# Another order of start, first batches and products in a graph layer kernel on one core

## The chip, the core and the metric

The kernel runs on one core of one Trainium2 chip. The metric is the device time of one execution in microseconds (us); smaller is better. The core has five engines that run beside one another and meet only at semaphores: TensorE (PE: matrix products and transposes, its weight loads shown as PEld), VectorE (DVE), ScalarE (ACT), GpSimd (POOL) and SyncE (SP), which here only starts transfers. ScalarE and GpSimd start transfers as well. A name with a q, as in SPq, is the queue of instructions of that engine.

## The reference

The input x has 32 batches of 512 tokens of 256 channels, and adj is a 512x512 mask for each batch. With h = relu(layernorm(x)), the layer computes

```
conv  = relu(h + bn2(conv17(relu(bn1(conv1x1(h))))))       # along the tokens
s     = h @ w_se.T + b_se                                   # 3 features a token
A     = exp(-|s_n - s_m|^2) * adj
nmp   = A @ relu(h @ w_msg.T + b_msg)
gi    = concat(conv, nmp) @ w_ih.T + b_ih ;  gh = h @ w_hh.T + b_hh
out   = x + GRU cell(gi, gh, h)
```

bn1 and bn2 are batch norms with given statistics, so each is one scale and one shift for a channel. All data are fp32.

## The kernel before

Batches are handled in two groups of 16 (GB = 16, NG = 2). The convolution of 17 taps is done in the frequency domain: windows of 64 tokens are turned into spectra of length 80, which gives UNITS = 40 units for each group, and a unit is a product of 128 windows by 256 channels with the transformed taps. The program has these stages in order.

**First part of group one** (`first_part(0, ...)`, up to about 174 us). For each batch: load x, `statistics` (mean and variance on VectorE, the power -0.5 on GpSimd, L290), `normalise` (VectorE, L296), `transpose_h` (TensorE transposes phT, L307, then VectorE writes hT with the relu, L308, and SyncE stores it), `conv1` (TensorE pc, L320; VectorE adds the shift, L323; ScalarE the relu, L324) and `windows_to_freq` (TensorE px, L335; ScalarE copies into xf, L338). Between these stand pieces of `weights_to_freq` (TensorE pw, L256; copies into wst on VectorE, L263, and ScalarE, L265), two for a batch, which transform the taps and store them in the DRAM tile WD, and one of `load_weights` for a batch. The last of these, `vectors`, forms the biases brz and the scale and shift of bn2 from the transfer vec2 that `load_vectors` started a batch before.

**Nodes of group one** (`nodes(0, ...)`, to about 469 us). It goes through the batches in the order `todo`. For each: `message` (TensorE pm, L431), `features` (VectorE, small), `factors` (TensorE transposes psl and psr, L450 and L455, copied by ScalarE), `affinity` (TensorE pd, L466; exp on ScalarE; transpose of adj and product on VectorE, L471 and L472) and `aggregate` (TensorE pn, L480). Units are spread among them: `product` (TensorE py, L385) needs the unit's weights wt (`load_unit`, L347, three buffers in the pool wts), their sum wsum (GpSimd, L351) and two combinations of the spectrum, both (GpSimd, L364 and L365). Its result y goes through ScalarE (L391) and VectorE (L392, L393) to DRAM. The last four units of group one (LEFT = 4), u0 to u3, are left for the next stage.

**First part of group two** (`first_part(1, ...)`, to about 590 us). The same steps for 16 more batches, without `weights_to_freq`. The four left units are done among its first batches: the list `left` has their steps, and each call of `fill()` takes one entry. `combine_weights` forms sums of the gate weights on GpSimd, one step a batch.

**Nodes of group two** (to about 891 us) is as in group one, with 40 units spread over 13 batches. **The gates**, from 891 us to the end, use pairs of batches and are not touched by the change.

The order of the instructions on each engine is what the program says where a stage stands under `tc.manual_schedule()`: the two first parts and the gates. In `nodes` the framework's scheduler puts the instructions of each engine in order. Every engine works through its own queue in that order, so an instruction that waits holds all that is behind it. PSUM has eight banks of 512 values, given out in turn by `bank()`; a product waits until whoever reads the bank's earlier contents is done.

The first batches of group one run on TensorE in this order (T transposes, C conv1, W a piece of weights_to_freq, F windows_to_freq; the number is the batch): T0 C0 W W T1, C1 T2 W F0 W, T3 C2 W F1 W, and so on. In group two: T0 u0 u1 C0 u2 T1 u3, T2 C1 F0, T3 C2 F1.

Of the kernel before, what the change touches and what calls it, by code (L numbers as in the profile page):

```python
# [11 lines left out]
FP = mybir.dt.float32  # L12
# [3 lines left out]
P = 128  # L16
# [49 lines left out]
def gnn_layer(  # L66
# [88 lines left out]
    def vectors():  # L155

        for h in range(2):
            rows = slice(64 * h, 64 * (h + 1))
            nc.vector.tensor_copy(vech[rows].rearrange("p (m e) -> p e m", e=DC),
                                  vec2[rows].rearrange("p e (m h) -> p e m h", h=2)[..., h])  # L160
        for name in VEC:
            at[name] = vech[:, cols[name]]
        nc.vector.tensor_add(brz, at["b_ih"][:, : 2 * DC], at["b_hh"][:, : 2 * DC])
        batch_norm("bn2", scale2, shift2, nc.vector)

    def batch_norm(k, scale, shift, engine):
        engine.tensor_scalar(scale, at[k + "_v"], BN_EPS, None, op0=ALU.add)
# [173 lines left out]

    WT, WSUM, BOTH = {}, {}, {}

    def load_unit(g, u):
        t = WT[g, u] = wts.tile([P, 2, DC, D], FP, tag="wt", name=f"wt_{g}_{u}")
        for k in range(2):
            nc.sync.dma_start(t[:, k], WD[2 * u + k, : D * D].rearrange("(p i o) -> p i o", i=DC, o=D))  # L347

# [150 lines left out]
    def combine_weights():  # L499

        steps = []
        for k, src in enumerate((w_hhT, w_ihT[D:], w_ihT[:D])):
            w, t = (pools["sums"].tile([P, n, 3 * P], FP, tag=f"w{n}", name=f"w{n}_{k}", bufs=m) for n, m in ((4, 1), (7, 2)))
            if k == 1:
                nc.sync.dma_start(w.rearrange("p (c h) m -> p c (h m)", c=DC), src.rearrange("(c p) m -> p c m", p=P))
            else:
                load_rows(w.rearrange("p (c h) m -> p c (h m)", c=DC), src, nc.sync)

            a11, a21, a12, a22 = (
                w[:, 2 * c : 2 * c + 2].rearrange("p h m -> p (h m)").rearrange("p (g i o) -> p g i o", i=2, o=32)[:, :, i]  # L510
                for c in range(DC) for i in range(2)
            )
            q = [t[:, n].rearrange("p (g o) -> p g o", o=32) for n in range(7)]
            for (dst, x1, x2, op), kept in zip(
                ((Q5, a21, a22, ALU.add), (Q6, q[Q5], a11, ALU.subtract),
                 (Q7, a11, a21, ALU.subtract), (Q3, a12, q[Q6], ALU.subtract)),
                ((Q1, a11), (Q2, a12), (Q4, a22), None),
            ):
                steps.append([partial(nc.gpsimd.tensor_tensor, q[dst], x1, x2, op=op)])
                if kept:  # L520
                    steps[-1].append(partial(nc.scalar.copy, q[kept[0]], kept[1]))
            steps[-1].append(partial(nc.sync.dma_start, WS[k], t.rearrange("p q (g o) -> p q g o", o=P)))
        return steps
# [275 lines left out]
    def first_part(g, freq, between, left=()):  # L799


        b0, b1 = g * GB, (g + 1) * GB
        for b in range(b0, b0 + 3):
            if b not in X and (g == 0 or b == b0):
                load_x(b)
        if g == 0:
            t = XN[b0] = pools["first"].tile([P, NC, D], FP, tag="xn", name="rows", bufs=2)
            ones, diags = t[:, 0, :P], t[:, 1:3, :].rearrange("p i (c m) -> p i c m", m=P)
            nc.vector.memset(ones, 1.0)
            batch_norm("bn1", scale1, shift1, nc.gpsimd)  # L810
            bn1_row(0, scale1, ones, diags)
            bn1_row(1, shift1, ones, diags)
        if b0 not in STATS:
            statistics(b0)
        normalise(b0)
        if g == 0:
            scale_w1()
            shift_w1()
        else:
            load_x(b0 + 1)  # L820
            load_x(b0 + 2)
        left = list(left)

        def fill():
            for step in left.pop(0) if left else ():
                step()

        fill()
        transpose_h(b0)
        fill()  # L830
        statistics(b0 + 1)
        normalise(b0 + 1)
        fill()
        for b in range(b0, b1):
            if b + 3 < b1:
                load_x(b + 3, nc.gpsimd)
            if b == b0:
                conv1(b)
                if g == 0:
                    for steps in between(0):  # L840
                        for step in steps:
                            step()
                fill()
            if g == 0 and b == b0 + 1:
                conv1(b)
            if b + 2 < b1:
                statistics(b + 2)
            if b + 1 < b1:
                transpose_h(b + 1)
            if b + 2 < b1:  # L850
                normalise(b + 2)
            if b == b0:
                fill()
                xf = freq(g)
            one, two = between(b - b0) if b > 0 else ([], [])
            if b > b0 + (g == 0):
                conv1(b)
            if b == b1 - 1:
                load_h(b0)
            for step in one:  # L860
                step()
            if b > b0:
                windows_to_freq(b - 1, xf)
            for step in two:
                step()
        by_chunks(b1 - 1)
        load_h(b0 + 1)
        windows_to_freq(b1 - 1, xf)
        by_chunks(b0)
        return xf  # L870
# [8 lines left out]
    with tc.tile_pool(name="freq", bufs=1) as fpool:  # L879
# [27 lines left out]
        def nodes(g, xf, units, last):  # L907


            b1 = (g + 1) * GB  # L910
            todo = [b1 - 1] + list(range(g * GB, b1 - 1))
            def begin(i):
                if i < GB:
                    if todo[i] not in HQ:
                        by_chunks(todo[i])
                    message(todo[i])
                    features(todo[i])

            load_adj(todo[0])
            begin(0)  # L920
            factors(todo[0])
            begin(1)
            affinity(todo[0])
            for i, b in enumerate(todo):
                mine = spread(units, i, last) if i < last else []
                more = i + 1 < GB

                if g + 1 < NG and i == GB // 2:
                    load_x(b1)
                if g + 1 < NG and i == 3 * GB // 4:  # L930
                    statistics(b1)
                if i + 2 < GB and todo[i + 2] not in HT:
                    load_h(todo[i + 2])
                if more:
                    load_adj(todo[i + 1])
                    factors(todo[i + 1])
                for u in mine[:1]:
                    product(pools["pw"], g, u, xf)
                begin(i + 2)
                if more:  # L940
                    affinity(todo[i + 1])
                for u in mine[1:2]:
                    product(pools["pw"], g, u, xf)
                aggregate(b)
                save_nmp(b)
                for u in mine[2:]:
                    product(pools["pw"], g, u, xf)

        with phase("pw", "ahead"):
            with phase("nodes"):  # L950
                nodes(0, xf, range(UNITS - LEFT), GB)
            with phase("first", "sums"):
                combine = combine_weights()

                def between(b):

                    if b == GB - 3:
                        for u in range(3):
                            load_unit(1, u)
                    two = [partial(sum_unit, pools["pw"], 1, b - GB + 3)] if b > GB - 3 else []  # L960
                    return combine[b - 2] if 1 < b < len(combine) + 2 else [], two


                pw, (u0, u1, u2, u3) = pools["pw"], range(UNITS - LEFT, UNITS)
                left = [[partial(load_unit, 0, u2)],
                        [partial(prepare, pw, 0, u1, xf), partial(product, pw, 0, u0, xf)],
                        [partial(product, pw, 0, u1, xf), partial(load_unit, 0, u3), partial(prepare, pw, 0, u2, xf)],
                        [partial(prepare, pw, 0, u3, xf), partial(product, pw, 0, u2, xf)],
                        [partial(product, pw, 0, u3, xf)]]
                prepare(pw, 0, u0, xf)  # L970
                load_unit(0, u1)
                with tc.manual_schedule():
                    xf = first_part(1, freq_tile, between, left)
            with phase("nodes"):
                nodes(1, xf, range(UNITS), GB - 3)
# [76 lines left out]
```

## Time and profile before

The median of three runs is 1853.91 us (1850.42 to 1854.76). The profiled execution has a span of 1857.3 us.

| stage | us of the span | PE idle in it, us | where |
|---|---|---|---|
| start to first conv1 | 0 to 11.5 | 8.1 | 7.24 before L187, 0.82 before L320 |
| rest of first part, group one | 11.5 to 174 | 4.9 | 2.12 at 20, 0.56 at 34, 1.82 and 0.32 at 88 to 92 |
| nodes, group one | 174 to 469 | 3.4 | all before 230 |
| first part, group two | 469 to 590 | 3.7 | 2.32 at 479, 1.35 at 489 |
| nodes, group two | 590 to 891 | 2.8 | 1.01 at 594, 0.71 at 607 |
| gates | 891 to 1857 | 9.5 | in the last 80 us |

The page has for each engine its busy time. The granted clock (PEclk) is a share of TensorE's full clock; it is 1.00 nearly everywhere. The timeline's columns are start, duration, engine, line, operation, output and inputs with their shapes, number of instructions, and in brackets how long the engine had been idle and what ended that wait. TensorE's matrix products of fp32 stand in the records twice each, and their durations overlap: a product with 512 columns takes 0.86 us by the distance of its neighbours.

### The profile page before, as it was taken

What the parts mean: (1) busy time and instruction counts of PE and PEld (TensorE: products, weight loads), DVE (VectorE), ACT (ScalarE), POOL (GpSimd) and SP (SyncE); (2) the same over time, 40 slices, a digit from 0 to 9 for tenths busy, and PEclk for the clock granted to TensorE, in tenths of its full rate; (3) what the DMA queues carried; (4) which work ended last, traced back from release to release, by engine and by line L of the source; (5) the groups of instructions that cost most, each with busy time, mean ns of one, the idle gap of its engine ahead of it and who ended that gap; (6) DMA issues with size and microseconds to landing.
All of it is one profiled execution on the core that took longest, in us unless ns stands there. A gap on an engine that the chain in (4) does not pass through costs nothing.

```text
span 1857.3 us, 20078 instructions
## 1 busy us (share of the span) xinstructions
PE 1824.6 (98%) x6598; PEld 1088.2 (59%) x6598; DVE 1112.3 (60%) x2234; ACT 578.5 (31%) x1075; POOL 587.3 (32%) x565
## 2 busy tenths in 40 slices
PE   7999999999999999999999999999999999999998
PEld 5667666666798667666555544555455544555443
DVE  7775565555696554555165566645665466645666
ACT  3455434342245433333222211222122212222121
POOL 3322243344442344444412322132213322132221
PEclk9989999999999999999999999999999999999999
DMA  8988989865677988768512442244422442244312
GB/s 227 296 244 239 219 231 252 214 185 180 202 240 209 240 244 243 220 199 249 159 61 58 119 119 85 42 111 119 113 65 61 119 119 85 41 112 119 110 25 52
DMA packets 307451, 289.25 MB, mean 156 GB/s; under 512 B 148028, under 2 KB 237148, under 8 KB 306964
## 3 DMA queue, kind: packets, MB, share of 16 engines
q1 hardware_dynamic: 281300, 224.22, 45.6%
q10 hardware_dynamic: 19024, 38.68, 5.8%
q0 software_dynamic: 7024, 25.07, 4.9%
q8 instruction: 53, 0.87, 0.2%
q14 instruction: 50, 0.41, 0.1%
HBM read 191.50 MB, written 96.40 MB: 155 GB/s over the span
## 4 chain that ended last, share of the span: by engine, by line
PE 91%; DVE 3%; DMA 3%; issue 2%; POOL 1%; ACT 1%; SPq 0%; POOLq 0%; ACTq 0%; DVEq 0%
PE pg L585 29%; PE pn L585 14%; PE pn L480 11%; PE py L385 11%; PE pc L320 5%; PE pm L431 5%; PE pc L573 5%; PE px L335 3%; PE pw L256 2%; PE pd L466 2%; PE phT L307 1%; DMA hT<-hd 1%; PE psr L455 1%; DMA nd<-nmp 0%; DVE stats L284 0%
## 5 line engine op out<-in xcount | busy, mean ns | idle before, releaser
L480 PE MATMUL pn<-A,msg 128*128 128x512 f32 x512 | 225.1, 593 | 0.0
L585 PE MATMUL pg<-hp,sw 128*128 128x512 f32 x434 | 221.8, 593 | 0.7 <-DVE rz L604 0.5
L585 PE MATMUL pg<-cp,sw 128*128 128x512 f32 x434 | 221.6, 592 | 0.0
L585 PE MATMUL pg<-np,sw 128*128 128x512 f32 x434 | 221.6, 592 | 0.0
L563 POOL TENSOR_TENSOR hp<-hp 128x512 f32<-128x512 f32 x64 | 81.0, 1276 | 412.9 <-DMA hp<-hd 263.9
L364 POOL TENSOR_TENSOR both<-xf 128x256 f32<-128x256 f32 x78 | 60.1, 771 | 326.6 <-PE py L385 293.3
L480 PEld LDWEIGHTS pn<-A,msg 128*128 128x128 f32 x512 | 97.3, 190 | 110.8 <-issue 107.7
L385 PE MATMUL py<-wt,both 128*128 128x256 f32 x624 | 152.8, 388 | 3.0 <-POOL both L365 2.3
L563 POOL TENSOR_TENSOR cp<-cp 128x512 f32<-128x512 f32 x64 | 80.5, 1269 | 233.8 <-ACT cp L579 232.5
L600 ACT ACTIVATE rz<-rz,brz 128x512 f32<-128x512 f32 x93 | 67.0, 721 | 260.2 <-DVE rz L604 260.2
L392 DVE TENSOR_TENSOR y<-y,py 128x256 f32<-128x256 f32 x78 | 31.8, 408 | 193.3 <-ACT y L391 191.0
L585 PEld LDWEIGHTS pg<-hp,sw 128*128 128x128 f32 x434 | 82.2, 190 | 104.8 <-issue 97.8
L585 PEld LDWEIGHTS pg<-np,sw 128*128 128x128 f32 x434 | 82.5, 190 | 103.8 <-issue 103.8
L585 PEld LDWEIGHTS pg<-cp,sw 128*128 128x128 f32 x434 | 82.5, 190 | 103.8 <-issue 103.8
L385 PEld LDWEIGHTS py<-wt,both 128*128 128x128 f32 x624 | 115.4, 192 | 46.1 <-issue 27.6
L472 DVE TENSOR_TENSOR A<-e,at 128x512 f32<-128x512 f32 x128 | 113.5, 925 | 33.2 <-ACT e L469 33.0
L351 POOL TENSOR_TENSOR wsum<-wt 128x512 f32<-128x512 f32 x78 | 109.5, 1405 | 54.0 <-DMA wt<-wd 44.6
L320 PE MATMUL pc<-w,hT 128*128 128x256 f32 x512 | 120.8, 391 | 2.9 <-DVE hT L308 2.9
L723 ACT ACTIVATE nt<-nt,vech 128x512 f32<-128x512 f32 x64 | 46.2, 722 | 235.8 <-DVE nt L722 235.8
L431 PE MATMUL pm<-wmsg,hq 128*128 128x259 f32 x512 | 117.6, 381 | 1.3 <-ACT hq L417 1.0
L585 PE MATMUL pn<-np,sw 128*128 128x512 f32 x224 | 114.4, 592 | 0.0
L585 PE MATMUL pn<-hp,sw 128*128 128x512 f32 x224 | 114.4, 592 | 0.0
(141 smaller groups left out, 2954.5 us busy)
## 6 DMA issues: line engine op xcount, KB each, us to landing
wt<-wd SPq DMA_DIRECT2D x160, 256.0 KB, 4.2
adj<-in_adj_dram SPq DMA_DIRECT2D x128, 256.0 KB, 5.8
wd<-wst SPq DMA_DIRECT2D x64, 320.0 KB, 5.3
yd<-y ACTq DMA_DIRECT2D x80, 256.0 KB, 4.4
yt<-yd SPq DMA_DIRECT2D x30, 640.0 KB, 7.3
hd<-hT SPq DMA_DIRECT2D x32, 512.0 KB, 4.2
nd<-nmp ACTq DMA_DIRECT2D x32, 512.0 KB, 3.5
xb<-in_x_dram SPq DMA_DIRECT2D x128, 128.0 KB, 3.8
```

The costliest lines, as they stand in the source:

```text
L320: nc.tensor.matmul(p[:, j, :], HT[b][:, ic, c * P : (c + 1) * P], w1[:, ic, :], start=(ic == 0), stop=(ic == DC - 1))
L335: nc.tensor.matmul(p[:, j * 2 * L : (j + 1) * 2 * L], H1[b][:, c0 + j, ic * P : (ic + 1) * P], fwd, start=True, stop=True)
L351: nc.gpsimd.tensor_tensor(t, WT[g, u][:, 0], WT[g, u][:, 1], op=ALU.add)
L364: nc.gpsimd.tensor_tensor(both[:, 0], re, im, op=ALU.add)
L385: nc.tensor.matmul(dst, v[:, ic, :], w[:, ic, :], start=(ic == 0), stop=(ic == DC - 1))
L431: nc.tensor.matmul(p[:, : D + NS], hq[:, ic, c * P : (c + 1) * P], wmsg[:, ic, :], start=(ic == 0), stop=(ic == DC - 1))
L472: nc.vector.tensor_mul(A[b][:, mc, :], e, at)
L480: nc.tensor.matmul(p, MSG[b][:, mc, dc * P : (dc + 1) * P], A[b][:, mc, :], start=(mc == 0), stop=(mc == NC - 1))
L563: nc.gpsimd.tensor_tensor(t[:, dst, :], t[:, a, :], t[:, b, :], op=sub)
L573: nc.tensor.matmul(bk[:, t0:t1], YT[p][j][:, c, oc * P : (oc + 1) * P], back[:, n : n + t1 - t0], start=(c == 0), stop=(c == len(spans) - ...
L585: nc.tensor.matmul(bk[:, t], sw[:, k, q, o, :], terms[k][q][:, t], start=(first and i == 0), stop=(i == len(ks) - 1), skip_group_check=True)
L600: nc.scalar.activation(rz[:, g, j, :], src, AF.Sigmoid, bias=brz[:, g : g + 1], scale=1.0)
```

## The change

It has five parts, all about the order of work:

- `vectors` runs on GpSimd instead of VectorE.
- In front of the first real products, six matrix products of constants (ident and the zero tile fr) are issued on TensorE; their result is overwritten.
- In the first two batches of group one, the pieces of `weights_to_freq` and the work on VectorE are put in another order: T0 C0 W T1, C1 W T2 W F0 W, and hT of batch 1 stands before the statistics of batch 2.
- In the first part of group two, the steps of the left units move: the third unit's weights get a tile in the pool sums and are loaded between two loads of x, it is prepared before the second unit's product, and conv1 stands ahead of the next batch's transposes from the second batch on. The loads of the gate weights become steps of their own in `combine_weights`, which then start one batch earlier.
- In `nodes`, the first unit's product stands between the first batch's message and factors, and the other units are spread as before.

All of it is meant to keep TensorE supplied in places where it waits, and to have its clock up when the real work starts. The same instructions run as before, but for the six products in front.

```diff
--- before.py
+++ after.py
@@ -156,12 +156,12 @@
 
         for h in range(2):
             rows = slice(64 * h, 64 * (h + 1))
-            nc.vector.tensor_copy(vech[rows].rearrange("p (m e) -> p e m", e=DC),
+            nc.gpsimd.tensor_copy(vech[rows].rearrange("p (m e) -> p e m", e=DC),
                                   vec2[rows].rearrange("p e (m h) -> p e m h", h=2)[..., h])
         for name in VEC:
             at[name] = vech[:, cols[name]]
-        nc.vector.tensor_add(brz, at["b_ih"][:, : 2 * DC], at["b_hh"][:, : 2 * DC])
-        batch_norm("bn2", scale2, shift2, nc.vector)
+        nc.gpsimd.tensor_add(brz, at["b_ih"][:, : 2 * DC], at["b_hh"][:, : 2 * DC])
+        batch_norm("bn2", scale2, shift2, nc.gpsimd)
 
     def batch_norm(k, scale, shift, engine):
         engine.tensor_scalar(scale, at[k + "_v"], BN_EPS, None, op0=ALU.add)
@@ -341,8 +341,8 @@
 
     WT, WSUM, BOTH = {}, {}, {}
 
-    def load_unit(g, u):
-        t = WT[g, u] = wts.tile([P, 2, DC, D], FP, tag="wt", name=f"wt_{g}_{u}")
+    def load_unit(g, u, pool=wts):
+        t = WT[g, u] = pool.tile([P, 2, DC, D], FP, tag="wt", name=f"wt_{g}_{u}")
         for k in range(2):
             nc.sync.dma_start(t[:, k], WD[2 * u + k, : D * D].rearrange("(p i o) -> p i o", i=DC, o=D))
 
@@ -501,10 +501,12 @@
         steps = []
         for k, src in enumerate((w_hhT, w_ihT[D:], w_ihT[:D])):
             w, t = (pools["sums"].tile([P, n, 3 * P], FP, tag=f"w{n}", name=f"w{n}_{k}", bufs=m) for n, m in ((4, 1), (7, 2)))
-            if k == 1:
-                nc.sync.dma_start(w.rearrange("p (c h) m -> p c (h m)", c=DC), src.rearrange("(c p) m -> p c m", p=P))
-            else:
-                load_rows(w.rearrange("p (c h) m -> p c (h m)", c=DC), src, nc.sync)
+            rows = w.rearrange("p (c h) m -> p c (h m)", c=DC)
+            load = (partial(nc.sync.dma_start, rows, src.rearrange("(c p) m -> p c m", p=P)) if k == 1 else
+                    partial(load_rows, rows, src, nc.sync))
+            if k == 0:
+                steps.append([])
+            steps[-1].append(load)
 
             a11, a21, a12, a22 = (
                 w[:, 2 * c : 2 * c + 2].rearrange("p h m -> p (h m)").rearrange("p (g i o) -> p g i o", i=2, o=32)[:, :, i]
@@ -807,6 +809,9 @@
             t = XN[b0] = pools["first"].tile([P, NC, D], FP, tag="xn", name="rows", bufs=2)
             ones, diags = t[:, 0, :P], t[:, 1:3, :].rearrange("p i (c m) -> p i c m", m=P)
             nc.vector.memset(ones, 1.0)
+
+            for _ in range(6):
+                nc.tensor.matmul(row1[1][:, : 2 * P], ident, fr.rearrange("p c g k -> p (c g k)")[:, : 2 * P], start=True, stop=True)
             batch_norm("bn1", scale1, shift1, nc.gpsimd)
             bn1_row(0, scale1, ones, diags)
             bn1_row(1, shift1, ones, diags)
@@ -816,16 +821,16 @@
         if g == 0:
             scale_w1()
             shift_w1()
-        else:
-            load_x(b0 + 1)
-            load_x(b0 + 2)
         left = list(left)
 
         def fill():
             for step in left.pop(0) if left else ():
                 step()
 
-        fill()
+        if g > 0:
+            load_x(b0 + 1)
+            fill()
+            load_x(b0 + 2)
         transpose_h(b0)
         fill()
         statistics(b0 + 1)
@@ -836,31 +841,37 @@
                 load_x(b + 3, nc.gpsimd)
             if b == b0:
                 conv1(b)
-                if g == 0:
-                    for steps in between(0):
-                        for step in steps:
-                            step()
+                one, two = between(0) if g == 0 else ([], [])
+                for step in one:
+                    step()
                 fill()
-            if g == 0 and b == b0 + 1:
+                transpose_h(b + 1)
+                statistics(b + 2)
+                normalise(b + 2)
+                fill()
+                xf, last_two = freq(g), two
+                continue
+            if g > 0 and b + 2 < b1:
+                statistics(b + 2)
+            if g > 0 or b == b0 + 1:
                 conv1(b)
-            if b + 2 < b1:
+            if b == b0 + 1:
+                for step in last_two:
+                    step()
+            if g == 0 and b + 2 < b1:
                 statistics(b + 2)
             if b + 1 < b1:
                 transpose_h(b + 1)
             if b + 2 < b1:
                 normalise(b + 2)
-            if b == b0:
-                fill()
-                xf = freq(g)
-            one, two = between(b - b0) if b > 0 else ([], [])
-            if b > b0 + (g == 0):
+            one, two = between(b - b0)
+            if g == 0 and b > b0 + 1:
                 conv1(b)
             if b == b1 - 1:
                 load_h(b0)
             for step in one:
                 step()
-            if b > b0:
-                windows_to_freq(b - 1, xf)
+            windows_to_freq(b - 1, xf)
             for step in two:
                 step()
         by_chunks(b1 - 1)
@@ -918,11 +929,12 @@
 
             load_adj(todo[0])
             begin(0)
+            product(pools["pw"], g, units[0], xf)
             factors(todo[0])
             begin(1)
             affinity(todo[0])
             for i, b in enumerate(todo):
-                mine = spread(units, i, last) if i < last else []
+                mine = spread(units[1:], i, last) if i < last else []
                 more = i + 1 < GB
 
                 if g + 1 < NG and i == GB // 2:
@@ -958,13 +970,13 @@
                         for u in range(3):
                             load_unit(1, u)
                     two = [partial(sum_unit, pools["pw"], 1, b - GB + 3)] if b > GB - 3 else []
-                    return combine[b - 2] if 1 < b < len(combine) + 2 else [], two
+                    return combine[b - 1] if 0 < b <= len(combine) else [], two
 
 
                 pw, (u0, u1, u2, u3) = pools["pw"], range(UNITS - LEFT, UNITS)
-                left = [[partial(load_unit, 0, u2)],
-                        [partial(prepare, pw, 0, u1, xf), partial(product, pw, 0, u0, xf)],
-                        [partial(product, pw, 0, u1, xf), partial(load_unit, 0, u3), partial(prepare, pw, 0, u2, xf)],
+                left = [[partial(load_unit, 0, u2, pools["sums"])],
+                        [partial(prepare, pw, 0, u1, xf), partial(product, pw, 0, u0, xf), partial(prepare, pw, 0, u2, xf)],
+                        [partial(product, pw, 0, u1, xf), partial(load_unit, 0, u3)],
                         [partial(prepare, pw, 0, u3, xf), partial(product, pw, 0, u2, xf)],
                         [partial(product, pw, 0, u3, xf)]]
                 prepare(pw, 0, u0, xf)
```

## The prediction

> **What bounds the kernel now.** I read the busy times first, then what TensorE waited for, then the waits one by one in the timeline.
>
> ```profile
> PE 1824.6 (98%) x6598; PEld 1088.2 (59%) x6598; DVE 1112.3 (60%) x2234; ACT 578.5 (31%) x1075; POOL 587.3 (32%) x565
> ```
>
> TensorE (PE) is busy for 98% of the span. Removing work from another engine brings nothing in itself; only the 32.7 us in which PE stands idle, and the stretches in which its clock is low, can be won. The list of PE's waits says where most of them are (columns: total us, times, longest):
>
> ```profile
> PE row L187 <- ACT rows L186: 7.2, 1, 7.2
> PE pc L320 <- DVE hT L308: 2.9, 2, 2.1
> PE py L385 <- POOL both L365: 2.3, 1, 2.3
> PE psl L450 <- DVE fr L445: 2.0, 2, 1.0
> PE px L335 <- DVE h L323: 1.8, 1, 1.8
> PE phT L307 <- DVE xn L296: 1.4, 1, 1.4
> PE pd L466 <- DVE y L392: 1.2, 1, 1.2
> ```
>
> A wait has a second price. In the windows of 1 us, the column PEclk (the granted clock) drops after such a gap:
>
> ```profile
> 21.00:22.00 1.00, 0.00 (x0) 0.00 (x0) 0.97 (x7) 0.00 (x0) 0.42 (x1) 0.50 1.04 135
> ...
> 89.00:90.00 1.00, 0.00 (x0) 0.00 (x0) 0.93 (x4) 0.00 (x0) 0.70 (x1) 1.00 0.86 352
> ...
> 93.00:94.00 1.00, 1.00 (x8) 0.76 (x7) 0.00 (x0) 0.78 (x4) 0.00 (x0) 0.50 0.00 0
> ```
>
> The clock is 0.50 from about 20.3 to 27.1 us and from 92 to 102.1 us. All engines but PE have slack on average, so the question is only which waits of PE go and which come.
>
> **The Trainium skill.** "TensorE: Matmul & The Clock Gate", Part 1, says that the clock is halved or restored by an activity window of about 3.4 us that runs free of the kernel. The trace agrees: the two low stretches last 6.8 and 10.1 us, two and three such windows. The same part calls ScalarE, VectorE and GpSimd strict first-in-first-out; the trace agrees, as VectorE stands at one instruction of L159 for 0.56 us while an addition for PE lies behind it. "GPSIMD Engine Reference", section 4.1, puts two-input elementwise work on GpSimd at about twice VectorE's time. For operands as small as these the trace shows less: 0.20 us on GpSimd (L169, at 4.69 us) against 0.16 on VectorE. "DMA: Bandwidth & Descriptors", section "Issuing engines are not separate DMA queues", says that all queues share 16 DMA engines; the DMA share of 1.0 and more between 160 and 240 us agrees. It matters for rival two.
>
> **Vectors on GpSimd.** The timeline around the largest loss:
>
> ```profile
> 87.29 0.17 DVE L159 COPY vech<-vec 64x28 f32<-64x28 f32 x1 [0.56 <-DMA vec<-in_vecs_dram]
> ...
> 87.71 0.18 DVE L159 COPY vech<-vec 64x28 f32<-64x28 f32 x1 [0.24 <-DMA vec<-in_vecs_dram]
> ...
> 89.45 1.29 DVE L323 TENSOR_TENSOR h<-pc,shift_row 128x512 f32<-128x512 f32 x2
> ...
> 90.19 1.41 PE L335 MATMUL px<-fwd,h 128*128 128x160 f32 x8 [1.82 <-DVE h L323]
> ```
>
> VectorE ended normalise at 86.73, waited for the transfer, for small operations and for GpSimd's power (0.81), and reached L323 at 89.45: 2.7 us late. PE ran out of free PSUM banks, idled 1.82 and then 0.32, and lost its clock for 10.1 us. The starts of transpose_h (phT) measure the whole: 72.42, 81.51, 96.36, 108.16, 118.42, 127.99, 137.73, 147.30, 156.95. Before the stall a batch takes 9.1 to 9.5 us (mean 9.3). From 81.51 to 156.95 there are seven batches in 75.4 us. Seven at 9.3 would be 65.1, a gain of 10.3; seven at the 9.6 that the later batches take would be 67.2, a gain of 8.2. I take 9.2 and keep both ends.
>
> On GpSimd the eight operations cost, by its rows at 3.58 to 5.44 us (0.22, 0.72, 0.20, 0.20, 0.20), five of the batch norm 1.6 us in total, and three more at 0.2 to 0.3 each some 0.8: 2.4 us, at most 4 if the copies of 64x28 cost as much as the 0.72 of a 128x256 addition. They start at 87.7 and end by about 90.2. Behind them in GpSimd's queue lie load_x(11), wanted two batches later, and the power of the next statistics (L290). Without the stall that power is due about 9.2 us after the last (84.30), so at 93.5. There are 3 us to spare, and the operations cost nothing.
>
> **Constant matmuls in front.** Six of N=256 are, by L320's cadence (16 records in 3.45 us, two to a matmul), 0.43 us each at full clock and 0.86 at half: 2.6 to 5.2 us. ident and fr are written by 1.75, so they end between 4.4 and 7.0, before 7.24, where PE starts now. L187's eight records take 2.08 us cold against 1.09 for eight warm ones of L307, so PE is ready 1 us sooner. But VectorE's scale_w1 waits for the DMA of w_in until 10.06, and hT follows it. First conv1 stays at 11.47. Gain 0.
>
> **First batches.** Now VectorE does h, three copies of wst, statistics(2) and only then hT of batch 1, which starts at 21.34; PE waits 2.12 from 20.05 and conv1(1) takes 6.17 us at half clock instead of 3.62. After the change hT comes before statistics and behind two copies of wst: VectorE is at 18.97, hT ends at 20.25, conv1(1) can start at about 19.8 instead of 22.17. A gap of some 2.4 us stays, so I do not count on a full clock. From there VectorE sets the pace, by its own durations: statistics with the power 2.9, normalise 1.4, h 1.3, wst 0.7 to 1.2, statistics 1.8, hT 1.3, normalise 1.4, wst 1.3. That puts wst of batch 1's first step at 32.5 to 33 and the transposes of batch 3 at about 33.1, against 35.21 now: gain 2.1, between 1.0 and 3.5 with the phase of the clock.
>
> **Group two, first part.** Its timeline has the third left product:
>
> ```profile
> 478.76 1.26 POOL L351 TENSOR_TENSOR wsum<-wt 128x512 f32<-128x512 f32 x1 [1.44 <-DMA wt<-wd]
> ...
> 481.45 3.52 PE L385 MATMUL py<-wt,both 128*128 128x256 f32 x8 [2.32 <-POOL both L365]
> ...
> 490.65 1.72 PE L307 MATMUL phT<-ident,xn 128*128 128x128 f32 x8 [1.35 <-DVE xn L296]
> ```
>
> Its weights were issued at 475.01, after SyncE's queue had waited 7.1 us. From a tile of their own in "sums", issued between two loads of x, they leave at about 467 to 468; even with 5.4 us to landing (the longest there) wsum and both end by 476, before PE's 479.13. PE then runs u2 (2.6) to 481.75, T (0.87) to 482.6, u3 to 485.2, conv1 (3.45) to 488.7. hT is ready at 484.3, the next normalise at about 488.4. T to 489.6 and windows_to_freq to 491.8 follow. The next hT ends at about 493.6, its first half at 493, so PE waits some 1.3 and conv1(18) starts at 493.1. Now the same work ends at 497.83: gain 4.7 us, the 2.32, the 1.35, some 2.3 of half clock, less the new gap. Bounds 3 to 6. In the steady batches PE needs 6.50 and VectorE 5.9 by their rows; with conv1 ahead of the transposes hT ends some 1 us before it is wanted, so nothing changes. The weights' first load, moved to batch 17, is wanted only a batch (6.5 us) later.
>
> **The product between messages and factors.** It fills PE's 1.01 us before psl, once in each group. In group two its weights are long there. In group one they leave SyncE at 175.04 and the second unit's arrive at 180.2, so the first's land near 179.2 while PE comes at 178.3: 0.1 us is won. Against that, every product stands one place earlier than its weights. Unit 3 in group one:
>
> ```profile
> 205.35 0.91 SPq L347 DMA_DIRECT2D wt<-wd  x2
> ...
> 211.25 1.27 POOL L351 TENSOR_TENSOR wsum<-wt 128x512 f32<-128x512 f32 x1 [5.15 <-DMA wt<-wd]
> ```
>
> Its product would be wanted at about 204.5 instead of 210.7: 2 to 5 us of new wait if the load stays there. On the other side 0.98, 1.17 and 1.7 us of half clock after 228 can go, since they come from the same late transfers. I take 0 for both groups together, with bounds of +4 and -8.
>
> **Sum.** 9.2 + 2.1 + 4.7 + 0 = 16.0; 1853.9 - 16.0 = 1837.9.
>
> **Rivals.** One, as worked out: 1838, chance 0.70. Two, the product order turns late transfers into new waits in both node stages (about 9 us lost): 1847, chance 0.16. For it speaks the DMA share above 1.0 there; against it the free places in PE's order later, where windows from 240 on are full. Three, GpSimd's wait takes the place of VectorE's: the transfer lands over 3 us later, L290 comes late and the stall stays. The gain of 9.2 is lost: 1847, chance 0.05. Against it: the landing at 87.7 leaves room. Four, the node stages lose step for several batches: 3 us of wait and half clock in each of four batches in both groups, 24 us, less 16: 1862, slower, chance 0.03. Five, also the gaps of the node stages go and the clock keeps up: 4 to 5 us more, 1833, chance 0.06.
>
> Case one spreads by its terms from 1834 to 1842, and two and three lie at 1847, so I give 1832.5 to 1847. Faster means below 1848.3: 0.93; within: 0.04; slower: 0.03.
>
> **What would show it.** Right: the phT starts between 80 and 100 us run at 9.1 to 9.6, with no clock of 0.50 there; L159 is on POOL and no wait of PE names h L323; PE's wait for both L365 is gone from group two, and its conv1 of the third batch starts 15 us or more sooner by the clock. Wrong: L290 waits behind L159 to L171; wt L347 lands after PE asks for it near 200 or 615 us; new waits of py for both or wt; the low clock near 20 us is longer than now. If the second half, from 877 us in the trace of before, takes more than now, none of this holds.

## The result and the profile after

The changed kernel takes 1855.6 us (median of 6 runs) against 1853.1 before: ratio 1.0016, interval 1.0000 to 1.0032. A later and longer series (a0_changed) has 1855.2 against 1851.8, ratio 1.0020 (1.0008 to 1.0033). The change costs some 3 us; the forecast was 16 us faster.

The page after, in its first part, reads almost as before:

```profile
PE 1824.9 (99%) x6610; PEld 1086.6 (59%) x6610; DVE 1104.3 (60%) x2227; ACT 578.8 (31%) x1075; POOL 587.5 (32%) x572
```

Its span is 1852.4 us, 4.9 shorter than the profiled execution of before, although the medians say the opposite. So one profiled execution need not be a usual one; the section on the prediction comes back to this. The list of TensorE's waits (total us, times, longest) shows what went and what came:

```profile
PE pc L320 <- DVE hT L308: 8.2, 6, 2.2
PE py L385 <- DMA wt<-wd: 2.6, 1, 2.6
PE row L814 <- DVE fr L224: 1.9, 1, 1.9
PE pd L466 <- ACT sr L457: 1.1, 1, 1.1
PE pd L466 <- DVE y L392: 0.9, 1, 0.9
```

Gone, as forecast, are the waits for h (L323), both (L365) and fr before psl (L445). New are a wait for a unit's weights and four more waits for hT; those for hT grew from 2.9 to 8.2 us.

The vectors, in GpSimd's timeline around 84 us:

```profile
83.43 0.33 POOL L159 COPY vech<-vec 64x28 f32<-64x28 f32 x1 [0.50 <-DMA vec<-in_vecs_dram]
84.73 0.21 POOL L159 COPY vech<-vec 64x28 f32<-64x28 f32 x1 [0.97 <-DMA vec<-in_vecs_dram]
...
87.07 0.84 POOL L118 DMA_DIRECT2D x<-in_x_dram  x1
...
92.42 1.03 POOL L290 TENSOR_TENSOR rstd<-rstd,minus_half 128x4 f32<-128x4 f32 x1 [4.51 <-DVE rstd L289]
```

They end at 87.1, load_x follows, and the power at 92.42 has waited for VectorE and not for them. This part does what it was meant to do.

The nodes of group one, TensorE's and SyncE's timelines:

```profile
194.21 0.60 PE L455 MATMUL psr<-ident,fr 128*128 128x128 f32 x4
197.39 2.86 PE L385 MATMUL py<-wt,both 128*128 128x256 f32 x8 [2.58 <-DMA wt<-wd]
...
207.31 1.79 PE L466 MATMUL pd<-sr,sl 9*128 9x512 f32 x4 [0.85 <-DVE y L392]
209.04 3.42 PE L385 MATMUL py<-wt,both 128*128 128x256 f32 x8
```

```profile
185.64 5.85 SPq L401 DMA_DIRECT2D adj<-in_adj_dram  x4
191.58 2.38 SPq L347 DMA_DIRECT2D wt<-wd  x4
```

Unit 3 is wanted at 194.8, when psr (194.21, 0.60 us) is done. Its weights stand in SyncE's queue behind the four transfers of a mask. The first of these waits until VectorE has read the buffer's earlier mask, at 185.6, and the last leaves by 191.5, so the weights leave at 191.58 and TensorE has them at 197.4. The products at 197.39 and 209.04 last 2.86 and 3.42 us instead of 1.89: the granted clock is 0.57 to 0.58 from 198 to 202 us and 0.51 to 0.64 from 208 to 212.

The first part of group two, SyncE, GpSimd, VectorE and TensorE:

```profile
513.78 0.36 SPq L873 DMA_DIRECT2D ws<-w  x1
514.56 0.82 SPq L873 DMA_DIRECT2D w<-in_w_ihT_dram  x1
```

```profile
524.12 1.00 POOL L873 TENSOR_TENSOR w<-w 128x384 f32<-128x384 f32 x1 [6.53 <-DMA w<-in_w_ihT_dram]
525.06 0.79 POOL L118 DMA_DIRECT2D x<-in_x_dram  x1
```

```profile
531.83 1.41 DVE L284 BATCH_NORM_STATS2 stats<-x 128x6 f32<-128x256 f32 x4 [2.73 <-DMA x<-in_x_dram]
```

```profile
535.58 3.89 PE L320 MATMUL pc<-w,hT 128*128 128x256 f32 x16 [1.63 <-DVE hT L308]
```

Read as a chain, these four are one event: the load of the second gate weights leaves behind a store of 1344 KB and lands 9.4 us later; GpSimd stands 6.53 us at the sum that needs it; load_x behind it is late; VectorE waits for x; TensorE waits for hT. In the kernel before, the load left first and the store second, the load landed after 4.8 us, and GpSimd's sum did not wait for it:

```profile
520.97 0.38 SPq L505 DMA_DIRECT2D w<-in_w_ihT_dram  x1
...
521.90 0.43 SPq L861 DMA_DIRECT2D ws<-w  x1
```

```profile
526.30 0.98 POOL L861 TENSOR_TENSOR w<-w 128x384 f32<-128x384 f32 x1
```

The sum was also wanted later there: 5.3 us after the load's issue, against 3.0 us in the changed kernel (GpSimd is free at 517.6).

### The profile page after: what moved, and what is told of

Same layout as the page of the kernel before. It is cut to its first block, busy times and chain, and to the rows that moved or that the text cites. A ratio compares the mean times of both kernels' runs of the same rounds, so it can differ in the third digit from the quotient of the medians.

```text
span 1852.4 us, 20108 instructions
## 1 busy us (share of the span) xinstructions
PE 1824.9 (99%) x6610; PEld 1086.6 (59%) x6610; DVE 1104.3 (60%) x2227; ACT 578.8 (31%) x1075; POOL 587.5 (32%) x572
## 4 chain that ended last, share of the span: by engine, by line
PE 88%; DMA 5%; DVE 3%; issue 2%; POOL 1%; SPq 0%; ACT 0%; POOLq 0%; ACTq 0%; DVEq 0%
PE pg L587 29%; PE pn L587 14%; PE pn L480 11%; PE py L385 10%; PE pm L431 5%; PE pc L575 5%; PE pc L320 4%; PE px L335 3%; PE pw L256 2%; PE pd L466 2%; PE phT L307 1%; DMA w<-in_w_ihT_dram 1%; DMA hT<-hd 1%; PE psr L455 1%; DMA x<-in_x_dram 1%
```

## The experiments

Theory one was that each part wins what its waits cost and two parts give it back: the early product in group one and the loads behind the stores. The rival was that the profile of before overstated what there was to win. Both hold in part. The e runs start from the kernel before, the a runs from the changed kernel; each ratio is against runs of the kernel before on the same chip. Each ratio has an interval of some 2 to 3 us either way, so a difference of 3 us between two of them is barely more than noise.

**e1_vectors**, the kernel before with one part of the change:

```diff
-            nc.vector.tensor_copy(vech[rows]...
+            nc.gpsimd.tensor_copy(vech[rows]...
...
-        batch_norm("bn2", scale2, shift2, nc.vector)
+        batch_norm("bn2", scale2, shift2, nc.gpsimd)
```

> The kernel before with only the vectors on GpSimd. Theory one (each part of the start brings what its waits in the profile cost, and later parts give it back): 6 to 9 us faster than before, and the transposes of the batches around 80 to 100 us at 9.1 to 9.6 us apart. Rival (the one execution profiled before the change had an unusually costly stall, with three windows of half clock, and a usual execution loses less there): 1 to 5 us faster by the times, though the trace shows the stall gone.

Measured: 1849.3 against 1851.8, ratio 0.9985 (0.9970 to 1.0000), some 2.8 us faster (0 to 5.6). TensorE's transposes and its pieces of weights_to_freq with the stall gone:

```profile
82.04 1.09 PE L307 MATMUL phT<-ident,xn 128*128 128x128 f32 x8
86.52 1.10 PE L256 MATMUL pw<-w2p,taps 17*80 17x512 f32 x8
89.92 2.57 PE L256 MATMUL pw<-w2p,taps 17*80 17x512 f32 x16
92.42 1.10 PE L307 MATMUL phT<-ident,xn 128*128 128x128 f32 x8
...
102.14 1.09 PE L307 MATMUL phT<-ident,xn 128*128 128x128 f32 x8
```

The batch still takes 10.4 us and the next 9.7. It holds 24 records of pw, not 16: 32 pieces spread over 15 batches make two batches with three pieces, and this is one of them. The rival's number is right.

**e2_first**, the kernel before with the new order of the first batches of group one only:

```diff
+            if g == 0:
...
+                    transpose_h(b + 1)
+                    statistics(b + 2)
+                    normalise(b + 2)
...
```

> The kernel before with only the new order of the first batches of group one (without the six products of constants). Theory one: some 2 us faster, the transposes of batch 3 at about 33 us instead of 35.2. Rival: the later work absorbs it, because the transfers after 160 us set the pace and not TensorE: no difference (within 1 us).

Measured: ratio 1.0002 (0.9988 to 1.0016), no difference. The transposes of batch 3 start at 34.18. In five profiles with the old order (before, e1, e3, e4 and e5_group2_loads below) they start at 32.67 to 35.75, mean 34.6; in nine with the new one at 32.80 to 34.74, mean 33.9. So 0.7 us is won there, less than one execution differs from another. Whether the later transfers absorb it, as the rival says, is not shown. The starts go with the low clock. Here is conv1(1), first in the profile of before, then in that of e4_product, which has the same order there, and a window in e4 (TensorE's clock is the number behind POOL's brackets):

```profile
22.17 6.17 PE L320 MATMUL pc<-w,hT 128*128 128x256 f32 x16 [2.12 <-DVE hT L308]
```

```profile
22.01 3.79 PE L320 MATMUL pc<-w,hT 128*128 128x256 f32 x16 [2.11 <-DVE hT L308]
```

```profile
21.00:22.00 1.00, 0.00 (x0) 0.03 (x1) 0.97 (x4) 0.00 (x0) 0.58 (x1) 1.00 1.09 131
```

Behind a wait of the same length the clock was at half for 6.8 us in the one execution and not at all in the other. The other old-order profiles have 3.5 (e3, e5) and 10 us (e1) of half clock there, and each of the nine with the new order still has at least one stretch of some 3.4 us between 12 and 36 us.

**e3_group2**, the kernel before with the first part of group two and the loads as steps:

```diff
+            steps[-1].append(load)
...
-                left = [[partial(load_unit, 0, u2)],
+                left = [[partial(load_unit, 0, u2, pools["sums"])],
...
```

> The kernel before with only the changes of the first part of group two (order, third left unit's weights in their own tile, gate weights' loads as steps). Theory one: the stage's beginning gains 2 to 4 us and its later batches lose 3 to 5, because each load of the gate weights now stands behind the store of 1344 KB in SyncE's queue, GpSimd waits for it, and load_x and the power of the statistics wait behind GpSimd: net 1 us faster to 2 slower, with waits of GpSimd for w of 8 us or more and waits of TensorE for hT of 1 us or more in the late batches. Rival (only the order conv1 before transposes is too tight): the waits for hT come in all batches, also without a wait of GpSimd before them.

Measured: ratio 1.0008 (0.9996 to 1.0020). TensorE waits for hT in three batches only (at 476, 486 and 559 us), so the rival, waits in all batches, falls. GpSimd's waits in this stage:

```profile
POOL w L871 <- DMA w<-in_w_ihT_dram: 14.5, 2, 8.3
```

This profile also shows the unchanged vectors on VectorE a second time:

```profile
80.52 1.09 PE L307 MATMUL phT<-ident,xn 128*128 128x128 f32 x8
...
88.73 1.41 PE L335 MATMUL px<-fwd,h 128*128 128x160 f32 x8 [1.35 <-DVE h L323]
90.46 2.86 PE L256 MATMUL pw<-w2p,taps 17*80 17x512 f32 x16 [0.32 <-ACT wst L265]
93.25 1.09 PE L307 MATMUL phT<-ident,xn 128*128 128x128 f32 x8
...
103.04 1.09 PE L307 MATMUL phT<-ident,xn 128*128 128x128 f32 x8
```

The same wait as before, but shorter (1.35 us, not 1.82), and the two batches take 22.5 us together instead of 26.7. The windows from 92 to 94 us, first of this kernel, then of the kernel before:

```profile
92.00:94.00 2.00, 2.00 (x16) 1.09 (x12) 1.61 (x3) 2.00 (x6) 0.00 (x0) 1.00 0.27 76
```

```profile
92.00:94.00 2.00, 2.00 (x10) 1.55 (x14) 0.00 (x0) 1.78 (x6) 0.00 (x0) 0.51 0.29 115
```

No low clock followed here. In e2, where the wait was 1.72 us, two low windows followed; in e4 and e5, where it was 0.95 and 0.94, none did. So at this place the longer waits went with low clock, and five profiles do not tell the length of the wait from chance. With the vectors on VectorE the two batches take 26.7 (before), 25.1 (e2), 22.5 (e3), 22.1 (e4) and 22.1 us (e5_group2_loads); with the vectors on GpSimd 20.1 (e1 and the changed kernel). So the stall costs 2.0 to 6.6 us, in three of the five profiles 2.0 to 2.4.

**e4_product**, the kernel before with the early product only:

```diff
+            product(pools["pw"], g, units[0], xf)
...
-                mine = spread(units, i, last) if i < last else []
+                mine = spread(units[1:], i, last) if i < last else []
```

> The kernel before with only the product between the first messages and factors of both groups. Theory one: unit 3 of group one is asked for before its weights have come: a new wait of 2 to 5 us with half clock behind it, 3 to 7 us slower in the nodes of group one; group two gains about 1 us. Net 2 to 6 us slower. Rival (the new wait only takes the place of the waits of before, since the same transfers set the pace): within 1 us of before.

Measured: 1858.6 against 1851.8, ratio 1.0036 (1.0025 to 1.0047), 6.7 us slower. Two waits stand in TensorE's timeline, a new one for unit 3 and, 10 us later, one for y, which the kernel before has with 1.17 us at 229:

```profile
199.42 1.97 PE L385 MATMUL py<-wt,both 128*128 128x256 f32 x8 [2.90 <-DMA wt<-wd]
209.90 1.59 PE L466 MATMUL pd<-sr,sl 9*128 9x512 f32 x4 [2.81 <-DVE y L392]
```

**a1_no_product**, the changed kernel with nodes as before (e4's diff undone).

> The changed kernel with nodes as before (no product between messages and factors, in neither group). Theory one (the early product of group one makes unit 3 wait for its weights): 5 to 8 us faster than the changed kernel, that is 2 to 5 us faster than the kernel before, and no wait of TensorE for wt near 200 us. Rival (the early start of the nodes stage, not the product, makes the weights late): the wait for wt stays and the time is that of the changed kernel within 2 us.

Measured: ratio 0.9999 (0.9988 to 1.0009), 3 to 4 us faster than the changed kernel's 1.0016 to 1.0020; no wait for wt is left, so the rival, that the early start of the stage makes the weights late, falls. The gain is below the 5 to 8 us expected.

**a2_load_first**, the changed kernel with

```diff
-            steps[-1].append(load)
+            steps[-1].insert(1, load)
```

> The changed kernel with one edit: each later load of the gate weights is issued ahead of the 1344 KB store of the sums before it, not behind. Theory one (the load waits behind the store, GpSimd waits for the load, load_x and the power wait behind GpSimd): GpSimd's two waits of 8 us for w fall to under 3 us, TensorE's waits for hT in the late batches of group two go, 1 to 3 us faster than the changed kernel. Rival (the order conv1 before transposes is too tight by itself): the waits for hT stay and the time does not move.

Measured: ratio 1.0001 (0.9990 to 1.0012), some 3 us faster than the changed kernel. GpSimd's longest wait for these loads is halved. It stays above the 3 us expected, but it reaches TensorE no more:

```profile
POOL w L873 <- DMA w<-in_w_ihT_dram: 7.8, 2, 4.2
```

From 500 to 590 us TensorE waits for nothing here; in the changed kernel it waits 2.8 us for hT in that stretch. The order conv1 before transposes is not too tight by itself. SyncE's queue shows the edit:

```profile
516.55 0.38 SPq L873 DMA_DIRECT2D w<-in_w_ihT_dram  x1
516.99 0.82 SPq L873 DMA_DIRECT2D ws<-w  x1
```

The load landed after 6.9 us. Over all profiles of these runs it takes 9.0 to 9.8 us behind the store (five), 6.8 to 7.9 ahead of it (five) and 4.8 to 5.2 in the old order (four).

**a3_both**, a2's edit and the product only in group two (`if g > 0:`).

> The changed kernel with both mended: the early product only in group two, and the gate weights' loads ahead of the stores. If both costs are what the single runs say (6.7 us for the product, 1 to 3 for the loads), 3 to 6 us faster than the kernel before. If they are one and the same lost time of the transfers, no more than 2 us faster.

Measured: 1844.8 against 1852.1, ratio 0.9961 (0.9947 to 0.9975), 7.2 us faster than before. This is more than expected.

**a4_no_warm**, the changed kernel without the six products of constants.

> The changed kernel without the six products of constants. If they only run in idle time and the first real work waits for the transfer of w1 anyway: within 1 us of the changed kernel, first conv1 at the same time. Rival (they keep the clock up at the start): 1 to 3 us slower, with half clock before 12 us. Other rival (they delay the first real products): up to 1 us faster.

Measured: ratio 1.0011 (1.0001 to 1.0020), against 1.0016 to 1.0020 with them: no difference that the intervals can tell. L187 runs 2.08 us without them and 1.21 to 1.38 with them (the granted clock reads 1.00 there in both, so the runs do not say why), but the first conv1 starts at 12.57 here, 12.16 in a3 and 11.09 in the changed kernel, each time after a wait for hT. No run shows that they help or hurt.

**a5_early_load**, a2's edit, the early product in both groups, and unit 3's load placed by hand:

```diff
             product(pools["pw"], g, units[0], xf)
+            load_unit(g, units[3])
```

> The changed kernel with the gate weights' loads ahead of the stores (as a2_load_first), the early product kept in both groups, and one more edit: unit 3's weights are issued directly after the first unit's product, in SyncE's queue ahead of the masks of the next two batches and not behind them. Theory one (only the place of unit 3's load in SyncE's queue makes the early product dear in group one): no wait of TensorE for wt near 195 us, 5 to 8 us faster than a2_load_first, so near a3_both. Rival (the transfers of that stretch are full, so an earlier load of unit 3 delays masks and tokens instead): the wait for wt goes but others of the same length come, within 3 us of a2_load_first.

Measured: 1844.9 against 1852.9, ratio 0.9949 (0.9931 to 0.9967), 9.5 us faster than before and level with a3. SyncE's queue and TensorE:

```profile
174.66 3.93 SPq L347 DMA_DIRECT2D wt<-wd  x2
179.34 4.78 SPq L401 DMA_DIRECT2D adj<-in_adj_dram  x4
```

```profile
196.69 1.89 PE L385 MATMUL py<-wt,both 128*128 128x256 f32 x8
```

The product of unit 3 starts without a wait. Between a2 and a5 there is one line, which acts in both groups, and about 9.6 us by the two ratios (intervals of 2 and 3 us, on two chips). The rival, that an earlier load would only delay others, falls.

**a6_old_nodes**, a2's edit and nodes as before in both groups.

> The changed kernel with the gate weights' loads ahead of the stores and nodes as before in both groups. It tells what the early product brings in group two alone, against a3_both, which has it there. Theory one: the product fills the 1.0 us before psl in group two, so this is 0.5 to 1.5 us slower than a3_both and 2 to 5 us faster than the kernel before. Rival (later units of group two then wait, as in group one): this is as fast as a3_both or faster.

Measured: ratio 0.9962 (0.9951 to 0.9973). Group two's early product (a3: 0.9961) makes no difference that can be told. Undoing the product where the loads are mended brings some 7 us, for group one alone (a2 1.0001, a3 0.9961) as for both (a6).

**e5_group2_loads**, e3 with a2's edit.

> The kernel before with only the changes of the first part of group two, and in them each later load of the gate weights ahead of the store of the sums before it. If the late loads were all that was wrong with this part, it now brings what its first batches win, 2 to 5 us faster than the kernel before, with TensorE's waits for hT only in the first three batches of the group. If the conv1 order or the third unit's tile costs something too, under 1 us.

Measured: ratio 0.9997 (0.9985 to 1.0009). By itself the mended part is worth 2 us against e3 and hardly anything against before, where 2 to 5 us were expected. The other theory's number, under 1 us, is the nearer one. From the first transposes of group two to the first aggregate (less 2.6 us where one more unit lies between) the old order takes 141.1, 141.3, 138.2 and 139.4 us in four profiles, the mended one 137.1, 137.5, 137.4, 137.4 and 138.9, and the one with the loads behind the stores 140.9 to 143.6 (five). By the means of the profiles the mended part wins 2.3 us on the old order and the late loads lose 1.9; the time here says a win of 0.6, between 2.8 and a loss of 1.7. What it is exactly stays open.

**a0_changed**, the changed kernel again.

> The changed kernel itself again, beside the same runs of the kernel before. All theories: 0 to 5 us slower than before, ratio 1.000 to 1.003; its spread tells how far the single differences of the other runs can be trusted.

Measured: ratio 1.0020 (1.0008 to 1.0033), with single runs from 1850.5 to 1863.7.

## Why the prediction was wrong

The forecast took case one; the run went the way of rival two, of which only the kind was foreseen: the early product made TensorE wait for late weights, but in group one alone. Of the signs of being right, no wait names h (L323) or both (L365) any more; but the batches between 80 and 100 us take 10.4 and 9.7 us and not 9.1 to 9.6, and conv1 of group two's third batch starts 10.7 us sooner and not 15 (488.00 against 498.71). Step by step:

- **The page: one execution taken for the usual one.** The mean granted clock of the profiled execution of before was 0.993, and it took 1859.1 us against a median of 1853. Of 59 runs of that kernel, 9 have a clock of 0.993 or less, 18 have 0.997; the 7 at 0.993 average 1856.2 us and the 18 at 0.997 average 1849.9. An estimate from the PEclk of windows of 10 us puts the half clock in that profile at 24 us, and in the profiles of e1 to e5 at 3 to 20 us. The savings were read from this page and taken off the median of 1853.9. The Trainium skill, "TensorE: Matmul & The Clock Gate", Part 1, says that the clock's activity window runs free of the kernel, and the runs fit this: waits of 2.12 and 2.11 us before conv1(1) brought two low windows or none. The work just ahead of them did not lie quite alike, so this is no proof. That sentence stood in the prediction; the conclusion from it, that the drop must be counted with a chance and not in full, was not drawn.
- **Vectors: 9.2 forecast, 2.8 measured (0 to 5.6).** The mechanism was right; the term was mis-sized in two ways. From the transposes of batch 8 on, the seven batches that were counted take 75.4 us before and 68.3 in e1, so the stall of that one execution was worth 7.1 us and not 9.2. The count "seven batches at 9.3" left out that one batch has three pieces of weights_to_freq and takes 10.4 us without any stall, and that the later ones take 9.6 to 9.7 anyway. The rest is clock: three windows of half clock were booked as the cost of the stall. In e3, e4 and e5, which have the stall without low clock, the same seven batches take 70.4 to 70.8 us, 2.1 to 2.5 more than without it.
- **Constant matmuls: 0 forecast, 0 measured.** Right, and for the reason given: the first conv1 waits for hT with and without them.
- **First batches: 2.1 forecast, 0.7 in the profiles, nothing in the times.** The end of the count was near (transposes of batch 3 at 33.1 forecast, 32.82 in the changed kernel's profile, 33.9 on average). The step that failed is its start: 35.21 holds two low windows, and the old order's average is 34.6. The new order's own low stretches were not sized.
- **Group two: 4.7 forecast, a loss of 1.5 us measured (interval from a gain of 0.7 to a loss of 3.7).** The wrong step is the sentence on the gate weights, "wanted only a batch (6.5 us) later". In the changed kernel the first load leaves at 488.98 and GpSimd is free for its sum at 492.8, 3.8 us later; it waits 4.27 us there. The second is wanted 3.0 us after its issue and stands behind a store of 1344 KB; GpSimd waits 6.53. The sentence asked in which batch a load is wanted, and not when SyncE's queue lets it go. The first batches were over-sized too: TensorE's 1.3 us before conv1(18) came as 1.43, but a wait of 0.83 us before conv1(17) was not in the working, and conv1(18) starts 25.9 us after the group's first transposes instead of 23.6. The half clock here was real: of the four old-order profiles before, e1 and e4 have some 3.4 us of it and e2 none, and none of the ten with the new order has any.
- **The product: 0 forecast with +4 to -8, 6.7 lost in e4.** This is the largest loss. The danger was named with its place and its wait (2 to 5 us; 2.4 to 2.9 came). The wrong step was to set the same late transfers' 0.98, 1.17 and 1.7 us against it, as though they would go in exchange. In e2, e3, a1, a3 and a6, without the early product, the 0.98 is always there, while the half clock is absent in all five and the 1.17 absent in four (0.81 in a3): what can go goes without the product. From the last transposes of group one to the third aggregate, less the extra unit, the five profiles with the early product and the late load average 80.2 us and the eight without the early product 75.8; a5, with the product and an early load, has 74.2. A reading was too high as well: the DMA share between 160 and 240 us is 0.77 to 1.15 by tens of microseconds, and not 1.0 and more throughout; in a5 an earlier load found room there.

The four parts measured singly sum to a ratio of 1.0031, against 1.0016 and 1.0020 together: the same within their intervals. Undone singly, product and loads bring about 3 us each; undone together 10 (a3). Likewise e1, e2 and e5, the parts that are left in a6 but for the constant products, sum to 0.9984, and a6 has 0.9962. Whether either is more than noise is open.

## What to carry to other kernels

Size a wait from several executions, and book a clock drop behind it as a chance; then count what the same stretch would take without the wait, with the work that really lies in it. When a product moves up one place, its load does not move with it: read the queue that issues the load, and what stands ahead of it there. Here two lines that moved loads ahead in SyncE's queue (a5) took the changed kernel from some 3 us slower than before to 9.5 us faster.

## What was not expected of the hardware

A load of 768 KB landed 9.0 to 9.8 us after its issue in the five profiles in which a store of 1344 KB stood ahead of it in SyncE's queue, 6.8 to 7.9 us in the five in which the store came directly behind it, and 4.8 to 5.2 us in the four of the old order. Why the last two groups differ is open. And a TensorE wait of 2.1 us at the same place of the program was followed by two low clock windows in one execution and by none in another. Between 10 and 40 us the time at half clock adds up to 0, 3.4, 6.8 or 10.2 us in all fourteen profiles, whole multiples of one window.
